# Attention's mean as a rank-one float32r product, and token numbers in buffers of their own, in a conv, attention and expert kernel

## The chip, the cores and the metric
The kernel runs on one core of a Trainium2 chip, in one launch. The metric is the device time of one execution in microseconds (us), as the median of several runs. The core's engines are TensorE (PE in the profile, with its weight loads as PEld), VectorE (DVE), ScalarE (ACT), GpSimd (POOL) and SyncE (SP, here a queue of DMAs). Each engine works through its own instructions in order, and they wait for each other by semaphores.

## What is computed
The input is x of shape (8, 56, 56, 256) in float32: 8 images of 3136 tokens with 256 channels. Cut to what matters:

```python
# layer 0: 32 paths of 1x1 conv (256 to 4), 3x3 conv (4 to 4), 1x1 conv (4 to 256), each with batch norm and relu
x = relu(sum_over_paths(conv3(conv2(conv1(x)))) + x)
# layer 1: attention with a matrix per image and head
t = x.reshape(8, 3136, 256)
n = (t - mean(t)) / sqrt(var(t) + 1e-5)           # over the 256 channels of a token
k = v = layernorm of n over each of 8 heads of 32 channels
kv = einsum('bhnd,bhne->bhde', k, v) / N
t = t + einsum('bhnd,bhde->bhne', n, kv) + n
# layer 1: mixture of 8 experts, 2 per token
n = (t - mean(t)) / sqrt(var(t) + 1e-5)
out = t + n + sum over the token's two experts of weight * (gelu(n @ w1[e] + b1[e]) @ w2[e] + b2[e])
```

The mean in the first normalisation is the one that the title speaks of: n = (t - mean) * r, so that n @ A = r * (t @ A - mean * (column sums of A)).

## The kernel before
The tokens go through in chunks: 7 chunks per image of 448 tokens each, 56 in all. A chunk is four groups of 112 tokens, which lie in 112 partitions. The work is a software pipeline over slots. Slot s holds the third conv of chunk s, the first conv of chunk s+2, the second conv of chunk s+1, the end of chunk s-1 (`end_steps`: transposes to tokens, head statistics, sums of k times v into `kvs`), the attention of chunk s-8 (`attn_steps`), the routing of tokens (`route_steps`) and some expert tiles (`moe_steps`). The instructions of PE, ACT and DVE are issued in an order written by hand: each step has a place between 0 and 1 in its slot (the table `places`, L614 on), and the steps of a slot are sorted by it. SP and POOL aren't in that list; their order follows from the program's.

In `end_steps`, `begin` stores the chunk channel-wise to DRAM (`tTs`) and `turn` stores it token-wise (`ts`). `variances` forms each token's statistics on DVE: `mu`, the sum of a token's eight head means, then `sd`, whose root POOL takes with a power (L793), or DVE by Newton steps in the last image. A slot before its attention, `fetch` brings `tT` and `X` back.

`image_steps` makes, once per image, the table `tab` that attention multiplies with: for each half f of the channels 256 columns of the image's matrix A plus the identity, with the column mean taken off, and 16 columns for the router. As A has blocks of 32x32 on its diagonal, half f has real entries in its own 128 columns; the other 128 hold only the negative column mean, which carries the token's mean.

`attend(k)` is attention for one group of 112 tokens: two matmuls into one PSUM tile (L983), then DVE scales and adds into X (L987), and ACT copies the 16 router columns to `lg` (L991):

```python
for f in range(NF):
    nc.tensor.matmul(ps, tT[:, f, k * T : (k + 1) * T], tables_of[b][:, f, :],
                     start=(f == 0), stop=(f == NF - 1))
```

The routed tokens are scattered by POOL as rows of 259 numbers (256 values, two weights, the token number) into DRAM regions by expert (L1163, `regions<-pay`). An expert tile is 256 such rows. `take_rows` loads them into a buffer `rows` of 8 (L1354, two tiles ahead), `take_weights` loads the expert's weights (L1364, one tile ahead, 4 buffers `w`), `tile_in` transposes (L1375) and names the token numbers in the rows buffer as the scatter's index, `tile_mid` and `tile_out` multiply (L1415, L1431, L1435), ACT writes `y` (L1439, 4 buffers), and `tile_add` lets POOL add the rows of y into the output at their token numbers (L1453, two scatters per tile). Only tiles that may be partial (the last 30 of 210) get an `index` tile of their own, made from the token numbers and a mask. After slot 56 there is no convolution any more; slots 57 to 64 hold attention of the last image with expert tiles, and then the remaining tiles follow.

A few names of size: T = 112, KT = 4, NF = 2, P = 128, C = 256, E = 8, CH = 448, HC = 32.

Of the kernel before, what the change touches and what calls it, by code (L numbers as in the profile page):

```python
# [8 lines left out]
F32 = mybir.dt.float32  # L9
# [16 lines left out]
def kernel(  # L26
# [30 lines left out]
    HC = 32  # L57
# [650 lines left out]
    def end_steps(s):  # L708
# [59 lines left out]
        def variances():  # L768
# [8 lines left out]
            dm = small([T, KT, NH], "hdm")  # L777
            nc.vector.tensor_reduce(mu, m, AX.X, ALU.add)
            nc.vector.scalar_tensor_tensor(
                dm, mu[:, :, None].to_broadcast([T, KT, NH]), -1.0 / NH, m,  # L780
# [63 lines left out]

    tables_of = {}

    def image_steps(b):
# [8 lines left out]
        def rows():  # L856
            v["kv"] = kvs.pop(b)

            v["rows"] = [
                one.tile([P, P], F32, tag=tag, name=f"{tag}_{b}") for tag in ("Arow", "At")  # L860
            ]
            for f in range(NF):
                nc.vector.tensor_scalar_mul(v["rows"][f], ident, ones_of(f))

        def along():
            ps = v["ps"] = ps_mm.tile([P, NF, P], F32, tag="mm", name=f"sv_{b}")
            for f in range(NF):
                nc.tensor.matmul(ps[:, f, :], ones_f, v["rows"][f], start=True, stop=True)
            v["A"] = one.tile([P, NF, P], F32, tag="A", name=f"A_{b}")

        def keys(f):
            A = v["A"][:, f, :]
            vw, vb = vw_b[:, f * P : (f + 1) * P], vb_b[:, f * P : (f + 1) * P]
            nc.vector.tensor_mul(A, v["kv"][:, f, f : f + P], vw)
            nc.vector.scalar_tensor_tensor(A, vb, ones_of(f), A, op0=ALU.mult, op1=ALU.add)
            nc.vector.tensor_scalar_mul(A, A, kw_c[:, f : f + 1])

        def values(f):  # L880
            A = v["A"][:, f, :]
            vw, vb = vw_b[:, f * P : (f + 1) * P], vb_b[:, f * P : (f + 1) * P]
            t = one.tile([P, P], F32, tag="At", name=f"At_{b}_{f}")
            nc.vector.tensor_mul(t, vw, v["ps"][:, f, :])
# [10 lines left out]
        def turn():  # L895
# [3 lines left out]
            for f in range(NF):  # L899
                nc.tensor.matmul(ps[:, f, :], mean_of, A[:, f, :], start=True, stop=True)  # L900
                nc.tensor.transpose(pt[:, f, :], A[:, f, :], ident)

        def matrix():
            A, ps = v["A"], v["cs"]
            AT = v["AT"] = one.tile([P, NF, P], F32, tag="AT", name=f"ATs_{b}")
            tab = v["tab"] = one.tile(
                [P, NF, C + 2 * E], F32, tag="tab", name=f"tab_{b}", bufs=2
            )
            nc.vector.tensor_copy(AT, v["pt"])
            for f in range(NF):  # L910
                for g in range(NF):
                    dst = tab[:, f, g * P : (g + 1) * P]
                    if f == g:
                        nc.vector.tensor_sub(dst, A[:, g, :], ps[:, g, :])
                    else:
                        nc.vector.tensor_scalar_mul(dst, ps[:, g, :], -1.0)
                nc.vector.tensor_copy(tab[:, f, C + E :], rwc[:, f, :])

# [19 lines left out]
        def centered():  # L938
            tab = v["tab"]
            for f in range(NF):  # L940
                nc.vector.tensor_sub(tab[:, f, C : C + E], v["AR"][:, f, :], v["pm"][:, :E])
            tables_of[b] = tab

# [7 lines left out]

    fetched, Xs, pays, logits = {}, {}, {}, {}

    def fetch(a):
        ts, tTs = spilled.pop(a)
        X = attn.tile([T, KT, C], F32, tag="X", name=f"X_{a}")
        tT = attn.tile([P, NF, CH], F32, tag="tT", name=f"tT_{a}")
        nc.sync.dma_start(out=tT, in_=tTs)
        nc.sync.dma_start(out=X, in_=ts)
        fetched[a] = tT  # L960
        Xs[a] = X

    def attn_steps(a):
# [15 lines left out]
        def attend(k):  # L979

            ps = ps_mm.tile([T, C + 2 * E], F32, tag="mm", name=f"at_{a}_{k}")
            for f in range(NF):
                nc.tensor.matmul(  # L983
                    ps, tT[:, f, k * T : (k + 1) * T], tables_of[b][:, f, :],
                    start=(f == 0), stop=(f == NF - 1),
                )
            nc.vector.scalar_tensor_tensor(  # L987
                X[:, k, :], ps[:, :C], rs1[:, k : k + 1], X[:, k, :],
                op0=ALU.mult, op1=ALU.add,
            )  # L990
            late.append(lambda: nc.scalar.copy(lg[:, k, :], ps[:, C:]))  # L991
            if k:
# [346 lines left out]
    def empty_rows(e):  # L1339
        pad = slots.tile([P, 2, ROW], F32, tag="rows", name=f"pad_{e}", bufs=8)  # L1340
        nc.gpsimd.memset(pad, 0.0)
# [8 lines left out]
    def take_rows(i):  # L1350
        row = entry(i, 0, E * CAPR - TR)
        z = slots.tile([P, 2, ROW], F32, tag="rows", name=f"rows_{i}", bufs=8)
        region = regions[slot_of[i][2]]
# [15 lines left out]
    def tile_in(i):  # L1369
# [12 lines left out]
        low = slot_of[i][3]  # L1382
        if low is not None:
            index = slots.tile([P, 2], I32, tag="index", name=f"index_{i}", bufs=12)
            past = slots.tile([P, 2], I32, tag="past", name=f"past_{i}", bufs=2)
# [278 lines left out]
```

## Time and profile before

| what | before |
|---|---|
| median of 3 runs | 3093.45 us (3087.57 to 3095.67) |
| the profiled execution | 3092.02 us |
| its span, first to last instruction | 3090.3 us |
| instructions | 53454 |
| mean granted TensorE clock | 0.972 |
| attention matmuls L983 | x896, 258.2 us busy |
| X update on DVE, L987 | x224, 476 ns median |
| rows loads and weight loads | x210 each, 259.0 and 513.0 KB |
| scatters of y, L1453 | x420 |

The times are of one execution. An instruction's duration in the profile is not its price on an engine that pipelines: PE's matmuls of some 400 ns overlap. What a group costs is read from the distance between starts, or from the chain of waits. A row of waits names the waiting instruction, what released it, the sum, the number of times and the longest.

### The profile page before, as it was taken

To read this page: it belongs to the slowest core of one execution; us is meant where nothing else is said; L and a number is where in the kernel's file an instruction comes from. 1 tells how busy PE (TensorE), PEld (TensorE's weight loads), DVE (VectorE), ACT (ScalarE), POOL (GpSimd) and SP (SyncE) were. 2 spreads that over 40 slices of the span, in tenths; PEclk is the share of its full clock that TensorE was granted. 3 is DMA by queue.
4 is the path that set the end of the run, shared out by engine and by line. 5 is a ranking of instruction groups with operands and counts; after the bars stand their busy time and mean duration, and the time that the engine had idled before them with its cause. 6 is when DMAs were issued, how large, how long until landed. Compare 5 with 4: busy or idle time off the path is not lost.

```text
span 3090.3 us, 53454 instructions
## 1 busy us (share of the span) xinstructions
PE 2875.4 (93%) x16677; PEld 1645.2 (53%) x16677; DVE 2124.4 (69%) x5532; ACT 1920.2 (62%) x3859; POOL 1800.1 (58%) x1333
## 2 busy tenths in 40 slices
PE   7999898888999999999999999999999997997798
PEld 3334443433455555555555555555555554776687
DVE  6877778788777777787777777787778784544000
ACT  4666566556666666667766666666666764554355
POOL 2332344445465765756766666576664556676677
PEclk8999999889999999999999999999999999998899
DMA  3534344436456777677776776767766666998897
GB/s 101 151 118 129 115 141 134 129 98 198 140 158 185 186 193 188 177 198 190 193 193 164 197 197 171 200 168 199 198 171 175 184 169 157 228 254 201 201 236 172
DMA packets 321708, 537.53 MB, mean 174 GB/s; under 512 B 40192, under 2 KB 231824, under 8 KB 321424
## 3 DMA queue, kind: packets, MB, share of 16 engines
q1 hardware_dynamic: 238464, 429.89, 45.6%
q0 software_dynamic: 82368, 103.47, 18.6%
q8 instruction: 133, 2.18, 0.3%
q14 instruction: 151, 1.24, 0.1%
q10 hardware_dynamic: 592, 0.76, 0.1%
HBM read 248.01 MB, written 192.55 MB: 143 GB/s over the span
## 4 chain that ended last, share of the span: by engine, by line
PE 72%; DVE 8%; ACT 6%; POOL 5%; DMA 5%; issue 4%; SPq 0%; ACTq 0%; POOLq 0%; DVEq 0%
PE c L660 14%; PE su L681 13%; PE ph L1415 11%; PE py L1435 9%; PE at L983 7%; PE kv L829 3%; PE c L324 3%; ACT r L665 3%; POOL hsd L793 3%; PE te L1375 3%; PE c L288 2%; DVE r L668 2%; PE py L1431 2%; DMA w<-Wd 2%; DMA out_dram<-y,rows 2%
## 5 line engine op out<-in xcount | busy, mean ns | idle before, releaser
L668 DVE SCALAR_TENSOR_TENSOR r<-c,nb,r 128x448 f32<-128x448 f32 x1792 | 1128.3, 677 | 401.2 <-ACT r L665 395.5
L665 ACT ACTIVATE r<-c,b3t 128x448 f32<-128x448 f32 x1792 | 1036.6, 634 | 342.6 <-PE c L660 338.1
L1453 POOL DMA_INDIRECT out_dram<-y,rows x360 | 567.0, 1575 | 415.6 <-ACT y L1439 262.8
L660 PE MATMUL c<-hl,W3hl 64*128 64x448 f32 x3584 | 684.9, 427 | 32.5 <-ACT r L665 18.7
L1163 POOL DMA_INDIRECT regions<-pay,rrowi x448 | 428.5, 957 | 308.9 <-PE c L660 172.8
L660 PEld LDWEIGHTS c<-hl,W3hl 64*128 64x128 f32 x3584 | 324.3, 188 | 490.6 <-issue 207.7
L681 PE MATMUL su<-r,gather 128*32 128x448 f32 x3584 | 532.2, 564 | 36.3 <-DVE r L668 32.5
L1415 PE MATMUL ph<-eT,w 128*128 128x256 f32 x1680 | 454.5, 402 | 40.2 <-DMA w<-Wd 24.0
L1439 ACT ACTIVATE y<-py,rows 128x256 f32<-128x256 f32 x420 | 196.9, 473 | 442.0 <-PE py L1435 364.9
L1435 PE MATMUL py<-w,hT 128*128 128x256 f32 x1680 | 432.8, 382 | 0.0
L1415 PEld LDWEIGHTS ph<-eT,w 128*128 128x128 f32 x1680 | 301.2, 194 | 173.0 <-issue 45.8
L793 POOL TENSOR_TENSOR hsd<-hsd,half 112x36 f32<-112x36 f32 x49 | 302.7, 6178 | 88.0 <-DVE hsd L791 84.1
L754 POOL TENSOR_TENSOR norm<-t,hmean 112x512 f32<-112x512 f32 x112 | 115.5, 1057 | 361.0 <-DVE hmean L743 220.9
L1419 ACT ACTIVATE hT<-ph,w 128x256 f32<-128x256 f32 x420 | 198.1, 476 | 187.7 <-PE ph L1415 130.9
L1435 PEld LDWEIGHTS py<-w,hT 128*128 128x128 f32 x1680 | 292.1, 192 | 29.3
L983 PE MATMUL at<-tab,tT 128*112 128x272 f32 x896 | 258.2, 411 | 7.1 <-ACT r L665 5.9
L681 PEld LDWEIGHTS su<-r,gather 128*32 128x32 f32 x3584 | 97.2, 109 | 218.7 <-issue 101.7
L1431 PE MATMUL py<-b2hl,own 128*128 128x256 f32 x420 | 182.2, 434 | 11.6 <-ACT lg L991 7.8
L983 PEld LDWEIGHTS at<-tab,tT 128*112 128x112 f32 x896 | 148.3, 179 | 81.5 <-issue 27.7
L987 DVE SCALAR_TENSOR_TENSOR X<-at,rs,X 112x256 f32<-112x256 f32 x224 | 107.0, 478 | 107.2 <-PE at L983 106.6
L1431 PEld LDWEIGHTS py<-b2hl,own 128*128 128x128 f32 x420 | 80.5, 192 | 141.8 <-issue 48.0
L324 PE MATMUL c<-R,W2t 96*32 96x448 f32 x1344 | 149.3, 546 | 0.1
(263 smaller groups left out, 3063.1 us busy)
## 6 DMA issues: line engine op xcount, KB each, us to landing
w<-Wd SPq DMA_DIRECT2D x210, 513.0 KB
rows<-regions SPq DMA_DIRECT2D x210, 259.0 KB
xi<-in_x_dram SPq DMA_DIRECT2D x56, 448.0 KB
hl<-hi SPq DMA_DIRECT2D x112, 224.0 KB
tTs<-xT SPq DMA_DIRECT2D x56, 448.0 KB
ts<-t SPq DMA_DIRECT2D x56, 448.0 KB
tT<-tTs SPq DMA_DIRECT2D x56, 448.0 KB
X<-ts SPq DMA_DIRECT2D x56, 448.0 KB
```

The costliest lines, as they stand in the source:

```text
L324: nc.tensor.matmul(ps[0][32 * g : 32 * g + 32, :CH], W2t[:, g, dy, :], R[:, g, :].rearrange("q (r w) -> q r w", w=W58)[:, dy : dy + ROWS, ...
L660: product = nc.tensor.matmul(tiles[g][:, :CH], W3hl[rows, ab, cg, :], hl[rows, ab, :], start=True, stop=True)
L665: nc.scalar.activation(r, tiles[0][:, :CH], AF.Relu, bias=b3t[:, cg, 2 * ab : 2 * ab + 1])
L668: nc.vector.scalar_tensor_tensor(r, tiles[1][:, :CH], nb3[:, cg, 2 * ab + 1 : 2 * ab + 2], r, op0=ALU.max, op1=ALU.add,)
L681: nc.tensor.matmul(ps[32 * c4 : 32 * c4 + 32, :CH], gather, unit.pop((s, 4 * u + c4)), start=(ab == 0), stop=(ab == NQ - 1),)
L793: nc.gpsimd.tensor_tensor(sd, sd, half[:T, :].rearrange("q (k h) -> q k h", k=KT), ALU.pow)
L983: nc.tensor.matmul(ps, tT[:, f, k * T : (k + 1) * T], tables_of[b][:, f, :], start=(f == 0), stop=(f == NF - 1),)
L1163: ins = nc.gpsimd.indirect_dma_start(out=regions[n], out_offset=bass.IndirectOffsetOnAxis(ap=v["row_i"][:, (m - group[0]) * KT + k, n : n ...
L1415: nc.tensor.matmul(ps, w[:, f * C + hf * P : f * C + (hf + 1) * P], eT[:, f, :], start=(f == 0), stop=(f == NF - 1),)
L1431: nc.tensor.matmul(ps, own.to_broadcast([P, P]), b2hl, start=True, stop=False)
L1435: nc.tensor.matmul(ps, hT[:, f, h * P : (h + 1) * P], w[:, (NF + f) * C : (NF + f + 1) * C], start=False, stop=(f == NF - 1),)
L1453: ins = nc.gpsimd.indirect_dma_start(out=out_rows, out_offset=at, in_=y[:, h, :], in_offset=None, compute_op=ALU.add, **partial,).ins
```

## The change
Attention's table is split. The mean's part becomes a product of its own: one float32r matmul whose stationary side holds, per token, the sum of head means as a rounded part and its remainder (`totals`, rows 0, 1, 32 and 33, all else zero), and whose moving side holds the negative column sums of A, rounded in rows 0 to 31 and the remainder in rows 32 to 63 (`less`, 272 columns with zeros under the router's). The rest of the table shrinks to 144 columns for each half: its own 128 and the router's 16. The two halves write overlapping stretches of the PSUM tile, columns 0 to 143 and 128 to 271, with the router's columns in the middle. `totals` are two buffers, zeroed once.

The rounded sums are made by DVE in `variances`, stored by SP to DRAM (`us`, 2 x 448, element by element as tokens lie across partitions), and loaded twice into `totals` by `fetch`.

In the tail, from slot 57 on, tiles that can't be partial get their token numbers copied by DVE to an `index` buffer (20 of them instead of 12), and the rows buffers go from 8 to 7.

```diff
@@ variances
             nc.vector.tensor_reduce(mu, m, AX.X, ALU.add)
+            mine = small([T, 2, KT], "hsum2")
+            nc.vector.tensor_copy(mine[:, 0, :].bitcast(F32R), mu)
+            nc.vector.tensor_tensor(
+                mine[:, 1, :].bitcast(F32R), mu, mine[:, 0, :], ALU.subtract
+            )
+            us = spill.tile([2, CH], F32, tag="us", name=f"us_{s}")
+            spilled[s] += (us,)
+            nc.sync.dma_start(out=us.rearrange("v (k q) -> q v k", q=T), in_=mine)
@@ image_steps
+    WT = P + 2 * E
+    WM = C + 2 * E
+    def router_of(tab, f):
+        return tab[:, f, P:] if f == 0 else tab[:, f, : 2 * E]
...
+            tab = v["tab"] = one.tile([P, NF, WT], F32, tag="tab", name=f"tab_{b}", bufs=2)
+            v["A"] = [tab[:, 0, :P], tab[:, 1, 2 * E :]]
...
             nc.vector.tensor_copy(AT, v["pt"])
+            less = v["less"] = one.tile([P, WM], F32R, tag="less", name=f"less_{b}", bufs=2)
             for f in range(NF):
-                for g in range(NF):
-                    dst = tab[:, f, g * P : (g + 1) * P]
-                    if f == g:
-                        nc.vector.tensor_sub(dst, A[:, g, :], ps[:, g, :])
-                    else:
-                        nc.vector.tensor_scalar_mul(dst, ps[:, g, :], -1.0)
-                nc.vector.tensor_copy(tab[:, f, C + E :], rwc[:, f, :])
+                mine = less[:, f * WT : f * WT + P]
+                nc.vector.tensor_scalar_mul(mine, ps[:, f, :], -float(HC))
+                nc.vector.scalar_tensor_tensor(
+                    mine[32:64], ps[32:64, f, :], -float(HC), mine[32:64].bitcast(F32),
+                    op0=ALU.mult, op1=ALU.subtract,
+                )
+                nc.vector.tensor_copy(router_of(tab, f)[:, E:], rwc[:, f, :])
+            nc.vector.tensor_scalar_mul(less[:, P:WT], ident[:, : 2 * E], 0.0)
@@ fetch
+    totals = [const.tile([P, CH], F32R, name=f"totals_{n}") for n in range(2)]
...
         nc.sync.dma_start(out=tT, in_=tTs)
         nc.sync.dma_start(out=X, in_=ts)
+        for n in range(2):
+            nc.sync.dma_start(
+                out=totals[a % 2][32 * n : 32 * n + 2, :].bitcast(F32), in_=us
+            )
@@ attend
-            ps = ps_mm.tile([T, C + 2 * E], F32, tag="mm", name=f"at_{a}_{k}")
+            ps = ps_mm.tile([T, 2 * WT], F32, tag="mm", name=f"at_{a}_{k}")
+            tab, less = tables_of[b]
+            nc.tensor.matmul(
+                ps[:, :WM], totals[a % 2][:, k * T : (k + 1) * T], less, start=True, stop=False
+            )
             for f in range(NF):
                 nc.tensor.matmul(
-                    ps, tT[:, f, k * T : (k + 1) * T], tables_of[b][:, f, :],
-                    start=(f == 0), stop=(f == NF - 1),
-                )
+                    ps[:, f * P : f * P + WT], tT[:, f, k * T : (k + 1) * T], tab[:, f, :],
+                    start=False, stop=(f == NF - 1),
+                )
+            mine = X[:, k, :].rearrange("q (f c) -> q f c", c=P)
             nc.vector.scalar_tensor_tensor(
-                X[:, k, :], ps[:, :C], rs1[:, k : k + 1], X[:, k, :],
-                op0=ALU.mult, op1=ALU.add,
-            )
-            late.append(lambda: nc.scalar.copy(lg[:, k, :], ps[:, C:]))
+                mine, ps.rearrange("q (f c) -> q f c", c=WT)[:, :, :P], rs1[:, k : k + 1],
+                mine, op0=ALU.mult, op1=ALU.add,
+            )
+            late.append(lambda: nc.scalar.copy(lg[:, k, :], ps[:, P:WT]))
@@ empty_rows, take_rows
-        z = slots.tile([P, 2, ROW], F32, tag="rows", name=f"rows_{i}", bufs=8)
+        z = slots.tile([P, 2, ROW], F32, tag="rows", name=f"rows_{i}", bufs=7)
@@ tile_in
         index = [z[:, h, C + 2 :].bitcast(I32) for h in range(2)]
         low = slot_of[i][3]
-        if low is not None:
-            index = slots.tile([P, 2], I32, tag="index", name=f"index_{i}", bufs=12)
+        if apart and low is None:
+            index = slots.tile([P, 2], I32, tag="index", name=f"index_{i}", bufs=20)
+            nc.vector.tensor_copy(index, z[:, :, C + 2].bitcast(I32))
+            index = [index[:, h : h + 1] for h in range(2)]
+        elif low is not None:
+            index = slots.tile([P, 2], I32, tag="index", name=f"index_{i}", bufs=20)
```

More of the change, by code (lines that the diff above doesn't have):

```diff
@@ L857, in rows @@
             v["kv"] = kvs.pop(b)
-            v["rows"] = [
-                one.tile([P, P], F32, tag=tag, name=f"{tag}_{b}") for tag in ("Arow", "At")
-            ]
+            AT = v["AT"] = one.tile([P, NF, P], F32, tag="AT", name=f"ATs_{b}")
             for f in range(NF):
-                nc.vector.tensor_scalar_mul(v["rows"][f], ident, ones_of(f))
+                nc.vector.tensor_scalar_mul(AT[:, f, :], ident, ones_of(f))
         def along():
@@ L867, in along @@
             for f in range(NF):
-                nc.tensor.matmul(ps[:, f, :], ones_f, v["rows"][f], start=True, stop=True)
-            v["A"] = one.tile([P, NF, P], F32, tag="A", name=f"A_{b}")
+                nc.tensor.matmul(ps[:, f, :], ones_f, v["AT"][:, f, :], start=True, stop=True)
+            tab = v["tab"] = one.tile([P, NF, WT], F32, tag="tab", name=f"tab_{b}", bufs=2)
+            v["A"] = [tab[:, 0, :P], tab[:, 1, 2 * E :]]
         def keys(f):
-            A = v["A"][:, f, :]
+            A = v["A"][f]
             vw, vb = vw_b[:, f * P : (f + 1) * P], vb_b[:, f * P : (f + 1) * P]
@@ L880, in values @@
         def values(f):
-            A = v["A"][:, f, :]
+            A = v["A"][f]
             vw, vb = vw_b[:, f * P : (f + 1) * P], vb_b[:, f * P : (f + 1) * P]
-            t = one.tile([P, P], F32, tag="At", name=f"At_{b}_{f}")
+            t = v["AT"][:, f, :]
             nc.vector.tensor_mul(t, vw, v["ps"][:, f, :])
@@ L899, in turn @@
             for f in range(NF):
-                nc.tensor.matmul(ps[:, f, :], mean_of, A[:, f, :], start=True, stop=True)
-                nc.tensor.transpose(pt[:, f, :], A[:, f, :], ident)
+                nc.tensor.matmul(ps[:, f, :], mean_of, A[f], start=True, stop=True)
+                nc.tensor.transpose(pt[:, f, :], A[f], ident)
         def matrix():
[L904 to L907, printed above, removed]
-            )
+            ps = v["cs"]
+            AT, tab = v["AT"], v["tab"]
             nc.vector.tensor_copy(AT, v["pt"])
+            less = v["less"] = one.tile([P, WM], F32R, tag="less", name=f"less_{b}", bufs=2)
             for f in range(NF):
-                for g in range(NF):
-                    dst = tab[:, f, g * P : (g + 1) * P]
-                    if f == g:
-                        nc.vector.tensor_sub(dst, A[:, g, :], ps[:, g, :])
-                    else:
-                        nc.vector.tensor_scalar_mul(dst, ps[:, g, :], -1.0)
-                nc.vector.tensor_copy(tab[:, f, C + E :], rwc[:, f, :])
+                mine = less[:, f * WT : f * WT + P]
[6 more added lines that the diff above has]
+            nc.vector.tensor_scalar_mul(less[:, P:WT], ident[:, : 2 * E], 0.0)
         def router():
@@ L940, in centered @@
             for f in range(NF):
-                nc.vector.tensor_sub(tab[:, f, C : C + E], v["AR"][:, f, :], v["pm"][:, :E])
-            tables_of[b] = tab
+                nc.vector.tensor_sub(
+                    router_of(tab, f)[:, :E], v["AR"][:, f, :], v["pm"][:, :E]
+                )
+            tables_of[b] = (tab, v["less"])
         return [
@@ L952 @@
     fetched, Xs, pays, logits = {}, {}, {}, {}
+    totals = [const.tile([P, CH], F32R, name=f"totals_{n}") for n in range(2)]
+    for t in totals:
+        nc.vector.tensor_scalar_mul(
+            t, ident[:, :1].to_broadcast([P, CH]), 0.0
+        )
     def fetch(a):
-        ts, tTs = spilled.pop(a)
+        ts, tTs, us = spilled.pop(a)
         X = attn.tile([T, KT, C], F32, tag="X", name=f"X_{a}")
@@ L1339, in empty_rows @@
     def empty_rows(e):
-        pad = slots.tile([P, 2, ROW], F32, tag="rows", name=f"pad_{e}", bufs=8)
+        pad = slots.tile([P, 2, ROW], F32, tag="rows", name=f"pad_{e}", bufs=7)
         nc.gpsimd.memset(pad, 0.0)
```

## The prediction
> **What bounds the kernel now.** I read the page first, then the busy time by stretch, the chain of waits in order of time, the waits of SP by stretch, and the timeline of single stalls. The first two lines below are the engines' shares and the granted clock from the page; the next are busy times by stretch (length; PE, PEld, DVE, ACT and POOL busy with their instruction counts; granted clock, DMA share, GB/s).
>
> ```profile
> PE 2875.4 (93%) x16677; PEld 1645.2 (53%) x16677; DVE 2124.4 (69%) x5532; ACT 1920.2 (62%) x3859; POOL 1800.1 (58%) x1333
> ...
> PEclk8999999889999999999999999999999999998899
> ...
> 300.00:800.00 500.00, 440.31 (x2508) 201.31 (x2508) 404.34 (x1005) 301.07 (x580) 221.50 (x154) 0.93 0.45 134
> ...
> 1500.00:2300.00 800.00, 784.39 (x4734) 434.42 (x4733) 603.94 (x1512) 539.12 (x1088) 523.85 (x361) 1.00 0.70 188
> ...
> 2870.00:2970.00 100.00, 87.31 (x415) 73.70 (x416) 2.61 (x16) 43.99 (x96) 67.28 (x48) 0.93 0.91 216
> 2640.00:2870.00 230.00, 196.15 (x1012) 167.30 (x1012) 106.38 (x486) 113.54 (x272) 162.46 (x126) 0.93 0.89 226
> 3000.00:3075.00 75.00, 75.00 (x400) 66.64 (x399) 4.79 (x29) 44.98 (x91) 58.56 (x39) 1.00 0.88 213
> ```
>
> There are four regimes. A slot is the stretch between the first L660 matmuls of two chunks. From about 829 to 2574 us (36 slots with conv, attention and expert tiles) PE has 98% and nothing else is above 76%: PE time is the time. From 304 to 829 (12 slots without tiles) PE idles 12% and loses clock. From 2640 to 2970 it idles 46.6 us of 330 at clock 0.93. From 3000 on it never idles.
>
> The chain of waits gives each group's length up to the next group's start, which is PE's real price (a matmul's own duration of some 400 ns is mostly pipeline depth):
>
> ```profile
> 2631.69 1.80 PE kv L829 x16
> 2713.59 0.92 PE at L983 x4
> 3002.03 0.12 PE py L1431
> 3004.43 1.73 PE ph L1415 x8
> ```
>
> A float32 matmul is two instructions. At 256 columns one costs 1.73/8 = 0.216 us, at 272 0.92/4 = 0.230, at 129 1.80/16 = 0.1125. The float32r matmul of 256 columns (L1431) is one instruction of 0.12.
>
> The tail's stalls start on SP's queue (waiter, what it waits for: us in all, times, longest), first for 2640 to 2840 and then from 2840 on; then POOL's scatters with start and duration:
>
> ```profile
> SPq L1354 <- DMA out_dram<-y,rows: 74.5, 19, 13.4
> ...
> SPq L1354 <- DMA out_dram<-y,rows: 88.1, 22, 10.6
> ...
> 2777.30 0.94 POOL L1163 DMA_INDIRECT regions<-pay,rrowi  x1 [0.30 <-DMA regions<-pay,rrowi]
> 2778.54 0.94 POOL L1163 DMA_INDIRECT regions<-pay,rrowi  x1 [0.30 <-issue]
> ...
> 2787.93 1.57 POOL L1453 DMA_INDIRECT out_dram<-y,rows  x1 [0.30 <-issue]
> 2789.80 1.57 POOL L1453 DMA_INDIRECT out_dram<-y,rows  x1 [0.30 <-issue]
> 2792.45 0.58 PE L1431 MATMUL py<-b2hl,own 128*128 128x256 f32 x1 [7.77 <-ACT lg L991]
> ```
>
> SP cannot load rows for tile n until the scatter of tile n-8 has landed, because that scatter reads its token numbers out of the rows buffer. The weights of a tile stand behind the rows on SP, so PE then waits for them. The last 30 tiles, which already have an index buffer of their own, run without such a wait at one tile in 4.13 us (3000.30 to 3004.43 in the chain).
>
> **The Trainium skill.** "FP8 and Floating Point Precision", TensorE Precision Notes: true FP32 takes four passes, a reduced form truncates the 4-byte value. "TensorE: Matmul & The Clock Gate", Back-to-back issue gap: N/2.4 + 2.5 ns a pass when warm. The trace agrees: two passes per instruction give 215.8, 229.2 and 110.0 ns against 216, 230 and 112.5 measured; one pass of 256 gives 109 against 120. The same page, LDWEIGHTS: columns/1.2 ns, so 93 ns for the 112 columns here, which a 122 ns matmul covers; kv's 128 weight columns under 129 moving ones show the cover. "DMA: Bandwidth & Descriptors", Specifications: below 512 B a transfer becomes a read-modify-write. The trace has 4-byte packets (19,824 on SP's queue, nearly all semaphore writes, median 9 ns) and one load of 4-byte elements (L470, 412 ns on SP), but no 4-byte data store.
>
> **The change, part by part.** The sums are made against the profiled execution, 3092.0 us with a span of 3090.3; the median of the runs is 1.4 above it.
>
> 1. PE in attend. Removed: 2 float32 matmuls of 272 columns, 0.92 us. Added: one float32r of 272, 0.12 x 272/256 = 0.128 us, and two float32 of 144, four instructions at 0.1125 x 144/129 = 0.126 (0.1225 by the skill's gap), so 0.49 to 0.50. Sum 0.62: 0.30 us less per attend, 1.2 per chunk, 67 over 56 chunks. Were float32r two passes, 0.11 more and 43 us in all; L1431 speaks against it. The extra first load of weights after a column-tiled group (0.92 becomes 1.10 at 1515.22 in the chain) is paid once before and once after.
>  By regime: 36 slots x 1.2 = 43; I take 90%, 39, since PE idles 2% there and shorter PE work opens a few waits. Slot 56: 1. The 12 early slots: 14 at most. There PE often waits for DVE's r (24.4 us, longest 5.2), behind DVE's own wait for POOL's root of hsd (58.9 us over the kernel), so I take 4. The 7 tail chunks (8 us) count in part 4.
>
> 2. The mean's road. DVE gets two 112x4 operations before that root, 0.17 + 0.03 us each by the neighbouring small rows: 0.4 us a slot, hidden behind PE with tiles, on the path in the early slots: -2 of the 12 x 0.4 = 5. SP gets the store of 896 elements of 4 bytes. It waits for DVE in `variances`; behind it on SP stand hl (which waited for DVE's hi 233.4 us anyway) and in about half the slots the next w and rows, then ph and te on PE. The L470 loads drew about 500 packets per us, so an estimate is 2 us; at 10 ns the engines give 896 x 10/16 = 0.6 us. hl follows on the same rings and has some 8 us to spare before the next slot needs it. Taken: 0; bounds 0 to a rival below. SP also gets two 1.8 KB loads per chunk into `totals`; the first attend waits for them, but they are issued a slot ahead beside tT. Their buffer is freed by attends two chunks back: 0. ACT's lg copy and DVE's X update keep size and count (the update's rows now lie 144 apart): 0, at most 224 x 0.05 = 11 on DVE, hidden except in the early slots.
>
> 3. The image steps swap 4 DVE operations of 128x128 for four others, 8 times: within 1 us, 0.
>
> 4. The tail. 51 tiles get an index copy (DVE has over half its time free there). The copy waits for rows that te needs at the same place, with attention's and the plan's DVE work behind it, which also waits for PE: 0 to -3, taken 0. Rows then go back when ACT has written y, 10 to 25 us before the scatter lands, by pairing each rows load from 2800 to 2930 with y and the scatter seven tiles earlier. So SP runs ahead, and w, the base's out store and the next X come earlier. What is late next: y has 4 buffers and also waits for the scatter (ACT 54.8 us, 13 times; the 7.77 us PE gap above is this, during eight regions scatters in a row), and POOL itself: an out scatter is 1.57 + 0.30 = 1.87 us, 3.74 a tile against PE's 4.13. With 0.30 per instruction POOL needs 162.5 + 38 = 200 of the 230 us and 67.3 + 14.4 = 82 of the 100. So at most 48 us can go, and at least the five w stalls after 2880 (1.66 + 2.46 + 1.27 + 1.47 + 1.27 = 8 us) should. I take half the ceiling, 25.
>
> 5. Rows buffers 8 to 7. The 129 tiles before the copies still free rows by the scatter. Up to slot 54 seven buffers leave 6 us or more between scatter issue and reuse, against some 3 us of landing; only around 2600 is one load held, about 12 us, 26 us ahead of its te. Bounds 0 to -8, taken -2.
>
> Sum: 39 + 1 + 4 - 2 + 25 - 2 = 65. 3092.0 - 65 = 3027; with the 1.4 to the median, 3028.
>
> **Rivals.**
> - The tail gives nothing: POOL's order of scatters, y and the last plan set it. For: POOL at 87% there, and the 7.77 us gap. Against: the SP waits of 162 us in all. Then 3093.4 - 40 = 3053.
> - PE's saving doesn't arrive: the loop PE, ACT, DVE over c and r paces a slot. For: DVE and ACT gain no time, and DVE is up to 0.88 of a slot. Against: slots at 0.2 us of PE idle. With a quarter of it and the tail, 3093.4 - 10 - 25 = 3058.
> - More than forecast: the tail reaches POOL's floor and the clock lost between 304 and 829 (39 us) partly comes back: 3093.4 - 44 - 48 - 12 = 2989.
> - Slower: the 4-byte stores. Each ring serves 56 per chunk in order, with hl behind them. Up to 8/56 = 143 ns each the slack takes it; above that every 10 ns is 0.56 us a slot, 31 us over 56 slots. At about 164 ns the 65 us are gone; at 180 ns the time is 3028 + 37 x 3.1 = 3143. For: no such store is in the trace, and the skill says it is read-modify-write. Against: 4-byte and 32-byte packets last 7 to 10 ns, 1 KB ones 46 to 58.
>
> **How the numbers follow.** Forecast 0.57, tail nothing 0.14, PE saving lost 0.12, more 0.09, slower 0.08. The forecast's own range is 3005 to 3050 (tail 5 to 45, early -8 to +12, main 32 to 43). To leave out no more than 2 in 10 the range takes in both middle rivals with their spread and the edge of the better one: 2995 to 3066. Less than 0.3% (9 us) can't be told from no change: faster 0.90, same 0.02 (where several of the gains fail together), slower 0.08.
>
> **What would show it.** Part 1: the float32r group of 224 at 0.12 to 0.13 us in the chain and at x4 at 0.50; the slots between 829 and 2574 shorter by about 1.1 us each. Part 2: SP's store of us near 0.5 us, its packets near 10 ns, hl not later. Part 4: no wait of the rows load for out_dram from the 130th tile on, PE idle from 2640 on well under 47 us, POOL over 90% there. I am wrong if the busy share of PE in the middle falls by as much as its work did, if the tail keeps its length while ACT's wait for y grows, or if 4-byte packets are over 140 ns.

## The result, and the profile after

The changed kernel takes 3074.67 us (median of 6 runs, 3071.33 to 3075.55) against 3094.56 of the kernel before on the same chip: ratio 0.9935, interval 0.9925 to 0.9945. The forecast was 65 us less, measured are 20. The profiled execution takes 3074.19 us, its span is 3072.3.

Busy time and instructions of each engine, from the page after:

```profile
PE 2842.7 (93%) x16901; PEld 1649.8 (54%) x16901; DVE 2143.1 (70%) x5705; ACT 1915.4 (62%) x3859; POOL 1798.8 (59%) x1333
```

The same view by stretch (length; PE, PEld, DVE, ACT, POOL busy with counts; clock, DMA share, GB/s):

```profile
300.00:800.00 500.00, 432.99 (x2540) 201.74 (x2536) 404.99 (x1016) 298.38 (x573) 218.32 (x152) 0.92 0.49 135
1500.00:2300.00 800.00, 780.02 (x4851) 439.38 (x4848) 614.56 (x1560) 544.85 (x1100) 526.72 (x363) 1.00 0.77 189
2640.00:2870.00 230.00, 199.18 (x1078) 173.70 (x1077) 94.80 (x476) 114.93 (x282) 166.45 (x130) 0.93 0.93 241
2870.00:2970.00 100.00, 88.75 (x430) 75.43 (x429) 11.59 (x46) 43.69 (x102) 68.55 (x46) 0.93 0.93 213
```

In the middle PE is busy 97.5% where it was 98%. Its work per slot fell by 2.5%, but its busy share hides most of what happened: the starts below show groups that take longer with little idle time in the record. In the tail PE idles 42 us of 330, where it idled 46.5, and the DMA share rose from 0.89 and 0.91 to 0.93. The mean granted clock is 0.968, where it was 0.972: the stretches below full clock, each counted by the share of speed that it lacks, cost 98.5 us in all, where they cost 87.5.

Where the time went is told by starts. The table is worked out from the first L660 matmul of slots 8, 20 and 55 in each trace (us):

| trace | up to slot 8 | slots 8 to 19 | slots 20 to 54 | from 55 to the end |
|---|---|---|---|---|
| before | 304.2 | 525.0 | 1697.3 | 563.8 |
| after | 307.0 | 529.2 | 1681.0 | 555.2 |
| difference | +2.8 | +4.2 | -16.3 | -8.6 |

The 35 slots of the middle were to bring 1.2 us each, 42. The distance from each matmul's start to the next one's, summed by group over these slots, shows what came of it: attend 134.5 to 104.6 us; the expert tiles' groups (te, ph, py, and pyb, which is py at L1431 before and L1463 after) 573.4 to 561.5, some 8 of these 12 in the distance to an attend that follows them. So the 42 us are there. The third convolution (c, L660) grew from 405.5 to 426.5 and su (L681, which sums its paths) from 272.6 to 277.6: 26 us came back.

Slot by slot the picture is steadier than these sums. In 32 of the 35 slots both traces have the full clock; there the change brings 0.47 us a slot on average, 15.2 in all, of the 1.2 that attend gives.

How the rest comes back is seen in the chain of waits, here in one slot, the same in both kernels. Before:

```profile
1548.85 0.92 PE tx L277 x8
1549.77 0.78 PE c L660 x4
1550.55 1.07 PE su L681 x8
1551.62 0.61 PE c L660 x4
1552.22 1.10 PE at L983 x4
1553.33 1.52 PE c L288 x4
...
1554.86 0.69 DVE r L668
...
1555.59 0.46 PE c L660
```

And after:

```profile
1519.68 0.12 PE at L1006
1519.81 0.49 PE at L1010 x4
...
1546.81 0.92 PE tx L277 x8
1547.72 0.80 PE c L660 x3
1548.52 0.67 ACT r L665
1549.25 0.57 issue
1549.82 0.68 DVE r L668
...
1551.15 0.60 DVE xT L687
...
1552.82 0.69 DVE r L668
1553.55 0.46 PE c L660
```

The price of attend is as forecast (0.12 for the float32r instruction and 0.49 for the four float32 ones). But from tx to the last c it is 6.74 us in both kernels: the chain now leaves PE for ScalarE's and VectorE's r, and what PE saves at the attend in between it waits longer for the last r. That r stands behind VectorE's own queue. These are the two r operations around it on VectorE (start, duration), before and then after:

```profile
1551.26 1.28 DVE L668 SCALAR_TENSOR_TENSOR r<-c,nb,r 128x448 f32<-128x448 f32 x2 [0.64 <-ACT r L665]
...
1554.86 1.27 DVE L668 SCALAR_TENSOR_TENSOR r<-c,nb,r 128x448 f32<-128x448 f32 x2
```

```profile
1549.22 1.28 DVE L668 SCALAR_TENSOR_TENSOR r<-c,nb,r 128x448 f32<-128x448 f32 x2 [0.64 <-ACT r L665]
...
1552.82 1.27 DVE L668 SCALAR_TENSOR_TENSOR r<-c,nb,r 128x448 f32<-128x448 f32 x2
```

In both kernels 3.60 us lie between them, and VectorE works without a gap there (nine router operations of 112x32, 112x64 and 112x8 and an xT of 128x448). PE's last c waits for that r in both, 0.16 us before and 0.46 after. So at this place VectorE's order of work sets the length, before the change too.

The wait that part 4 wanted gone is gone. SP's queue, first 2640 to 2840, then from 2840 on (waiter, cause: us, times, longest):

```profile
SPq L1382 <- DMA out_dram<-y,rows: 6.8, 2, 4.9
...
SPq L1382 <- ACT y L1471: 9.9, 6, 2.9
```

The wait of the rows load for scatters was 162.6 us before (from 2640 on) and is 6.8 now. Of ACT's waits from 2640 on, the one for y's buffers, before and then after:

```profile
ACT y L1439 <- DMA out_dram<-y,rows: 54.8, 13, 12.2
```

```profile
ACT y L1471 <- DMA out_dram<-y,index: 100.1, 25, 11.2
```

It has nearly doubled: rows run ahead, and y stands in their place. Both sizes belong to this trace: in e5 and e6 below, the same two kernels on another chip, the rows' wait is 57.5 and then 5.7 us, and y's 14.5 and then 32.7.

### The profile page after: what moved, and what is told of

Its sections match the earlier page's. It is cut to its first block, busy times and chain, and to the rows that moved or that the text cites. A ratio compares the mean times of both kernels' runs of the same rounds, so it can differ in the third digit from the quotient of the medians.

```text
span 3072.3 us, 54367 instructions
## 1 busy us (share of the span) xinstructions
PE 2842.7 (93%) x16901; PEld 1649.8 (54%) x16901; DVE 2143.1 (70%) x5705; ACT 1915.4 (62%) x3859; POOL 1798.8 (59%) x1333
## 4 chain that ended last, share of the span: by engine, by line
PE 39%; DVE 4%; DMA 3%; ACT 3%; POOL 3%; issue 3%; POOLq 0%; ACTq 0%; DVEq 0%; SPq 0%
PE ph L1447 8%; PE py L1467 7%; PE c L660 6%; PE su L681 6%; DMA out_dram<-y,index 3%; PE te L1403 2%; PE py L1463 2%; PE at L1010 2%; PE c L324 2%; PE kv L837 1%; POOL regions L1191 1%; DVE r L668 1%; ACT r L665 1%; POOL out_dram L1485 1%; ACT y L1471 1%
## 5 line engine op out<-in xcount | busy, mean ns | idle before, releaser
L660 PE MATMUL c<-hl,W3hl 64*128 64x448 f32 x3584 | 700.7, 430 | 36.4 <-ACT r L665 19.8
L1485 POOL DMA_INDIRECT out_dram<-y,rows x258 | 408.0, 1582 | 318.4 <-ACT y L1471 243.1
L660 PEld LDWEIGHTS c<-hl,W3hl 64*128 64x128 f32 x3584 | 331.2, 188 | 488.9 <-issue 215.5
L681 PE MATMUL su<-r,gather 128*32 128x448 f32 x3584 | 540.5, 566 | 43.4 <-DVE r L668 33.6
L1485 POOL DMA_INDIRECT out_dram<-y,index x162 | 251.0, 1549 | 94.1 <-issue 26.5
L681 PEld LDWEIGHTS su<-r,gather 128*32 128x32 f32 x3584 | 99.4, 109 | 231.2 <-DVE r L668 106.1
L1463 PE MATMUL py<-b2hl,own 128*128 128x256 f32 x420 | 175.1, 417 | 16.7 <-ACT y L1471 7.7
L1463 PEld LDWEIGHTS py<-b2hl,own 128*128 128x128 f32 x420 | 80.0, 190 | 145.4 <-issue 48.9
L1403 PE MATMUL te<-ident,rows 128*128 128x128 f32 x840 | 135.2, 284 | 19.4 <-ACT y L1471 18.4
```

The source lines that it names most:

```text
L660: product = nc.tensor.matmul(tiles[g][:, :CH], W3hl[rows, ab, cg, :], hl[rows, ab, :], start=True, stop=True)
L681: nc.tensor.matmul(ps[32 * c4 : 32 * c4 + 32, :CH], gather, unit.pop((s, 4 * u + c4)), start=(ab == 0), stop=(ab == NQ - 1),)
L1463: nc.tensor.matmul(ps, own.to_broadcast([P, P]), b2hl, start=True, stop=False)
L1485: ins = nc.gpsimd.indirect_dma_start(out=out_rows, out_offset=at, in_=y[:, h, :], in_offset=None, compute_op=ALU.add, **partial,).ins
```

## The experiments

The runs came in five groups, each on one chip with the kernel before beside it. Its median was 3103.9 us for e1 to e4, 3109.1 for e5 to e8, 3094.4 for e9 to e12, 3104.1 for e13 to e16 and 3109.5 for e17 and e18. Ratios are against these; stretches are compared within a group where that is possible. The second and the fourth group ran on the same chip. Where slots of the middle are compared one by one, only those count in which both traces have the full clock.

**Half of the change at a time.** e1 takes the index copies back, e2 everything but them and the 7 rows buffers.

```diff
-        if apart and low is None:
-            index = slots.tile([P, 2], I32, tag="index", name=f"index_{i}", bufs=20)
-            nc.vector.tensor_copy(index, z[:, :, C + 2].bitcast(I32))
```

> The mean product with its road, rows buffers 7, without the index copies of the tail. Theory (DVE paces the middle: of the 43 us that PE saves between 829 and 2574 us, 17 arrive; early slots lose 4; the tail part is worth 8): 8 us above the changed kernel, so about 3083, ratio 0.996 to before. Rival (the tail's copies gave nothing and the 8 us in the tail are the 7 chunks' shorter matmuls): 3075, as the changed kernel.

> Before with only the index copies and rows buffers 7. Theory: the middle as before, the tail's wait moves from the rows load to y's four buffers; 5 to 10 us off, 3084 to 3089. Rival (the copies are what gave the whole 20 us, the mean product nothing): 3075.

Measured: e1 3103.05 us, 1.0002 (0.9992 to 1.0011); e2 3104.74, 1.0004 (0.9995 to 1.0013). The middle is 1687.5 in e1 and 1699.3 in e2, so the mean's product does bring 12 us there; the time from slot 55 on is 573.3 and 577.0, where the first pair of traces had 563.8 and 555.2. Neither half alone moved the time of the whole. Neither the kernel before nor the whole change was traced on this chip, so these tails have no reference of their own. In e2 the rows' wait for scatters from 2640 on is down to 2.2 us, and the whole is no faster: the wait that part 4 wanted gone can go without any gain.

**The mean's road.** e3 leaves out the store and the loads of the mean's sums; e4 has the two DVE operations and the store in `inverse`, after the root.

```diff
@@ e3
-            nc.sync.dma_start(out=us.rearrange("v (k q) -> q v k", q=T), in_=mine)
...
-        for n in range(2):
-            nc.sync.dma_start(
-                out=totals[a % 2][32 * n : 32 * n + 2, :].bitcast(F32), in_=us
-            )
@@ e4, in inverse
+            nc.vector.tensor_copy(mine[:, 0, :].bitcast(F32R), total)
+            nc.vector.tensor_tensor(
+                mine[:, 1, :].bitcast(F32R), total, mine[:, 0, :], ALU.subtract
+            )
+            nc.sync.dma_start(out=v["us"].rearrange("v (k q) -> q v k", q=T), in_=mine)
```

> The changed kernel without the store of us and the two loads of totals (totals stay zero, so the token's mean is left out); DVE's two operations stay. Theory (DVE): within 3 us of the changed kernel, 3072 to 3078, though the DMA share of the middle falls back from 0.77 to about 0.70 and the mean of a 4104-byte packet from 239 to about 210 ns. Rival (the 4-byte stores slow the loads and so the slots): 10 us or more faster than the changed kernel, 3065 or less.

> The changed kernel with DVE's two operations and the store of us moved from before POOL's root to behind it, where DVE waits for POOL anyway. Theory (the two operations delay r by 0.36 us a slot and start the root later): 0.2 to 0.3 us in each of 36 slots and 0.3 in the 12 early ones, 9 to 14 us faster than the changed kernel, 3061 to 3066; the sixth su group and the c group before the second half of conv2 return to their lengths of before. Rival (DMA contention, or PE itself): no change, 3072 to 3078.

Measured: e3 3092.4, 0.9971 (0.9958 to 0.9983); e4 3113.91, 1.0043 (1.0027 to 1.0059). Without the road the middle stays at 1689.0 against e1's 1687.5, so the store costs nothing there. From slot 55 on e3 takes 565.0 against 573.3, but it has the index copies that e1 lacks, so that difference isn't the road's alone. In e4 the middle is 1705.7, 18 us longer than in e1. Nearly all of that is clock: the stretches below full clock cost 22.2 us there, and 5.1 in e1; what lowered the clock isn't shown. In the 23 slots with full clock in both, the typical (median) slot is 0.27 us shorter than in e1, as the theory said (0.2 to 0.3), although single slots are up to 2.6 longer and the mean is only 0.10. So the two operations do cost something in front of the root, and the store pays for their new place: it stands on SP until the root is done, with hl and xi behind it, and PE waits 11.8 us for hl, all of it ahead of slot 20.

**The two kernels again, the operations left out, and VectorE relieved.** e5 is the kernel before, e6 the changed one. e7 stores a constant in place of the two DVE operations' result; e8 halves two reductions.

```diff
@@ e7
-            nc.vector.tensor_copy(mine[:, 0, :].bitcast(F32R), mu)
-            nc.vector.tensor_tensor(
-                mine[:, 1, :].bitcast(F32R), mu, mine[:, 0, :], ALU.subtract
-            )
+            mine = nothing
@@ e8, also for the means
-                ss, v["sq"].rearrange("q k (h c) -> q (k h) c", c=HC), AX.X, ALU.add
+                ss, v["sq"].rearrange("q k (h c) -> q (k h) c", c=HC)[:, :, : HC // 2],
+                AX.X, ALU.add
```

> The kernel before, unchanged, as a traced reference on the same chip as the next three. Ratio 1.000. Every theory: middle (slots 20 to 54) 1697 us, early slots 525; only the tail may differ from the first trace, by some 10 us, if chips differ in how fast scatters and loads land.

> The changed kernel, unchanged, as a traced reference. If the two parts add, and the mean product alone and the tail's copies alone each gave nothing on that chip, the ratio is 1.000 there; if they need each other (the copies only help once PE is ahead of POOL), 0.994 as at first. Middle 1681, early 529.

> The changed kernel without DVE's two operations in variances; the store of us sends a tile of zeros instead (the token's mean is left out), so SP no longer waits there for DVE. Theory (DVE is the second bound and the two operations are its overflow): 0.36 us in most middle slots, so the middle 1668 to 1672 instead of 1681 and the c group before conv2's second half shorter; early 525; 10 to 15 us faster than the changed kernel. Rival (the give-back has nothing to do with these two): within 3 us of the changed kernel.

> The changed kernel with DVE's two long reductions per chunk (head sums and squares, 1.21 us each) over half of each head's channels, so the statistics are not the reference's; 1.2 us of DVE time per slot less, nothing else. Theory (DVE is what takes back PE's saving in the middle): c and su groups shrink by most of the 26 us they gained, middle about 1660, 20 us or more faster than the changed kernel. Rival (ACT's half of the loop, or DMA): middle unchanged within 4 us.

Measured: e5 1.0006 (0.9993 to 1.0018); e6 3100.98, 0.9974 (0.9962 to 0.9985), so on this chip the change is worth 8 us; e7 3221.7, 1.0373 (1.0347 to 1.0398); e8 3064.11, 0.9864 (0.9848 to 0.9879). The middle: 1702.5, 1691.2, 1681.7, 1670.0.

e7's stores have nothing to wait for, so SP ran them ahead, and this priced them by themselves. SP's queue (start, duration), then what PE waited for up to slot 8, then the DMA's packets while these stores ran:

```profile
69.26 49.77 SPq L784 DMA_DIRECT2D us<-nothing  x15
```

```profile
PE c L660 <- DMA hl<-h: 115.3, 4, 40.4
```

```profile
DMA packets 14545, 0.09 MB, mean 2 GB/s; under 512 B 14542, under 2 KB 14542, under 8 KB 14542
```

15 stores of 896 elements in 49.77 us are 3.3 us a store, or 59 ns an element on each of 16 rings, and PE waited 115.3 us for hl behind such stores; e7 reaches slot 8 134 us later than e6. e7's middle is 9.5 us under e6's, and the typical slot 0.26 us shorter, as in e4. This fits a price of the two operations (0.33 us of VectorE), but e7 also took SP's wait away.

**One chip for the operations and y's buffers.** e9 is the changed kernel; e10 is the kernel before with e8's relief; e11 has y in 5 buffers and rows in 6; e12 has the two operations on GpSimd.

```diff
@@ e11
-            hidden[i].append(work.tile([P, 2, C], F32, tag="y", name=f"y_{i}", bufs=4))
+            hidden[i].append(work.tile([P, 2, C], F32, tag="y", name=f"y_{i}", bufs=5))
@@ e12
-            nc.vector.tensor_copy(mine[:, 0, :].bitcast(F32R), mu)
-            nc.vector.tensor_tensor(
+            nc.gpsimd.tensor_copy(mine[:, 0, :].bitcast(F32R), mu)
+            nc.gpsimd.tensor_tensor(
```

> The changed kernel, unaltered, as the reference of this group: its ratio to the kernel before was 0.9935 in the first comparison and 0.9974 on another chip. Here 0.993 to 0.998. In the middle (the 35 slots 20 to 54, between first matmuls of the first convolution) 1681 to 1692 us.

> The kernel before, with the two DVE reductions over 1024 elements of a chunk (sums and sums of squares per head) reduced to half their elements, as in e8 on the changed kernel; the output differs. DVE work falls by 2 x 0.53 us a slot. With it the four cases with and without the change, and with and without the relief of DVE, are complete. Theory (DVE is a second bound in the middle, and takes what PE gives): in the kernel before, PE is the later one, so the relief brings little there: middle 0 to 10 us shorter than the kernel before's 1697 to 1703, so that between this kernel and e8 (1670) lie 25 to 35 us, most of the 42 that the price of attend promises; whole kernel 0.995 to 1.000. Rival (the relief shortens a chain in either kernel alike, and the lost saving is lost to something else, as slower transfers): middle 21 us shorter here too, ratio 0.989 to 0.992.

> The changed kernel with y in 5 buffers instead of 4, rows in 6 instead of 7 (for room), and the index copies for all tiles (by GpSimd ahead of the tail, by VectorE in it). Theory (in the tail the wait for rows was replaced by ACT's wait for a free y, 100 us in 25 waits from 2640 on): that wait falls to under half, PE's waits for te and py fall, and the stretch from slot 55 to the end becomes 5 to 15 us shorter than in e9. Rival (GpSimd's scatters pace the tail, whatever buffers there are): the wait moves to another place and the stretch stays within 3 us.

> The changed kernel with the two added operations of 112x4 in variances on GpSimd instead of VectorE, ahead of GpSimd's root of hsd, for which it waits about 2.8 us there. The store waits for GpSimd then. Theory (DVE's two operations cost some 9.5 us in the middle and 4 early, since DVE is the second bound): if GpSimd does both in under 2.8 us, the middle is 7 to 11 us shorter than e9 and the early slots 2 to 4. If GpSimd takes longer than it has, the root of hsd is later by the excess, the early slots lose 12 times the excess, and the middle gains less. Rival (the cost was the store's, not the operations'): no shorter than e9 anywhere.

Measured: e9 3074.49, 0.9934 (0.9921 to 0.9946), with the stretches of the first trace within 1 us; e10 3076.14, 0.9941 (0.9929 to 0.9953), between the ranges of theory and rival, middle 1696.4 in an execution that is the slowest of its six (3085.76); e11 3122.25, 1.0087 (1.0073 to 1.0102); e12 3075.56, 0.9944 (0.9927 to 0.9961), middle 1680.0 against e9's 1681.0.

GpSimd did both operations of e12 in the gap ahead of its root (start, duration, operation):

```profile
1770.13 0.21 POOL L780 CAST hsum<-hmu 112x4 fp32r<-112x4 f32 x1 [1.34 <-DVE hmu L778]
1770.42 0.20 POOL L781 TENSOR_TENSOR hsum<-hmu,hsum 112x4 fp32r<-112x4 f32 x1
1771.33 6.14 POOL L802 TENSOR_TENSOR hsd<-hsd,half 112x36 f32<-112x36 f32 x1 [0.71 <-DVE hsd L800]
```

So VectorE was rid of 0.33 us a slot, and the middle gained 1 us (0.02 in the typical slot): the theory's 7 to 11 failed here, and the two operations' price in the middle lies between 1 us (e12) and 9.5 (e7). Why GpSimd doing them gives back what e4 and e7 gained isn't shown. Slots 8 to 19 lost 3.0, with 8.5 us more lost to the clock, and the stretch ahead of them gained 2.8.

In e11 the copies for all tiles, which GpSimd makes in the slots, held up other work there: the middle is 1709.3, and PE waits 14.3 us in it for GpSimd's norm. The tail can still be looked at. ACT's wait for y from 2640 on, e9 and then e11:

```profile
ACT y L1471 <- DMA out_dram<-y,index: 124.6, 31, 11.1
```

```profile
ACT y L1471 <- DMA out_dram<-y,index: 104.7, 25, 9.7
```

A fifth buffer takes 20 us off the wait, and the stretch from slot 55 on is not shorter (562.2 against 555.6). As rows have one buffer less at the same time, this says only that the trade brought nothing, not that y's buffers are no limit.

**ScalarE's share, and the DMA engines in the tail.** e13 is the changed kernel, e14 is e8 again, e15 halves ScalarE's squares as well, e16 has every second tail tile use its neighbour's weights.

```diff
@@ e15
-                    sq[:, :, f * P : (f + 1) * P], norm[:, :, f * (P + 1) : f * (P + 1) + P],
+                    sq[:, :, f * P : (f + 1) * P].rearrange("q k (h c) -> q k h c", c=HC)[
+                        :, :, :, : HC // 2
+                    ],
+                    heads(norm)[f][:, :, :, : HC // 2],
@@ e16
+        if apart and i % 2 and i - 1 in weights_of:
+            weights_of[i] = weights_of[i - 1]
+            return
         e = entry(i, 1, E - 1)
```

> The changed kernel, unaltered, as the reference on this chip: middle (slots 20 to 54) 1681 to 1692 us, from slot 55 to the end 555 to 573.

> The changed kernel with VectorE's two reductions over 1024 elements halved, as in e8; the output differs. Theory (VectorE is the second bound in the middle once attend is shorter): middle 15 to 21 us shorter than e13, where the kernel before lost only 1 us by the same relief (e10). Rival (e8's gain was the chip's): middle within 4 us of e13.

> As e14, and ScalarE's squares over the halves that are used only (two operations a slot, 0.63 us each, to about 0.4); the output differs. Theory A (what e14 leaves of the lost saving is ScalarE's, which reads c before VectorE does): the third convolution shortens by 5 us or more against e14, toward the kernel before's 405 us. Theory B (the rest is the length of the loop PE, ScalarE, VectorE, PE itself, which shorter work in between no longer covers, however much time these engines have): within 3 us of e14 in the middle.

> The changed kernel, but in the tail every second tile takes its neighbour's weights in place of loading its own 513 KB; the output differs. GpSimd's, ScalarE's and PE's instructions stay. Theory (the DMA engines are what holds the tail now: share 0.93 from 2640 to 2870): the stretch from slot 55 to the end 15 us shorter or more, y's buffers come free sooner since the scatters land sooner, ACT's wait for y at under 70 us (from 100 to 125), and the middle unchanged. Rival (order and number of GpSimd's scatters): that stretch within 5 us, ACT's wait for y as it was, DMA share down to 0.75 to 0.8.

Measured: e13 3095.94, 0.9977 (0.9969 to 0.9985); e14 3060.88, 0.9864 (0.9837 to 0.9890); e15 3071.57, 0.9889 (0.9868 to 0.9911); e16 3086.13, 0.9941 (0.9925 to 0.9956). The middle: 1689.4, 1668.9, 1669.4, 1689.4. ScalarE's squares are worth nothing there, though the relief is small: ScalarE is busy 32.6 us a slot in e14 and 32.3 in e15. In e16 the stretch from slot 55 on is 7.3 us shorter (566.2 to 558.9), between the two theories. One stretch of the tail, e13 and then e16:

```profile
2840.00:2940.00 100.00, 82.10 (x406) 69.51 (x405) 28.38 (x130) 42.69 (x97) 71.94 (x56) 0.88 0.87 216
```

```profile
2840.00:2940.00 100.00, 86.76 (x429) 73.88 (x428) 29.44 (x132) 46.80 (x102) 71.77 (x55) 0.90 0.76 169
```

The DMA share falls by 0.11, PE does 6% more in the same time, and GpSimd is as busy as before. ACT's wait for y from 2640 on is 41.9 us in e13 and 20.8 in e16. The clock is a rival in this pair of traces: from slot 55 on 49.2 us are lost to it in e13 and 40.5 in e16, more than the 7.3. Over all runs it is not: e16 is 10 us faster by the medians, and the mean clocks, 0.9648 and 0.9654, are worth some 2 us. So the transfers hold a part of the tail, not all.

**The relief with and without the change on one chip.** e17 is e10's kernel, e18 is e8's.

> As e10: the kernel before with VectorE's two reductions halved; the output differs. Theory (VectorE became late through the change): less gain than e18 over e13 in the middle, 0 to 5 us below the kernel before's 1697 (on a chip with 3094 us for the kernel before) or 1702 (3104 to 3109). Rival: 15 us or more below.

> As e14: the changed kernel with the same relief; the output differs. Theory: middle 25 to 35 us shorter than e17, in place of the 12 to 16 that the change brings there without the relief, and the whole 15 us or more below e17. Rival: 12 to 16 us in the middle, as without the relief.

Measured: e17 3097.07, 0.9960 (0.9947 to 0.9973); e18 3078.28, 0.9896 (0.9869 to 0.9922). The middle is 1696.2 and 1675.7. With VectorE relieved the change brings 20.5 us there, and 19 in the whole (the medians' difference). Without the relief it brought 16.3 in the first pair and 11.3 between e5 and e6. By slots with full clock it is 0.63 us a slot with the relief, and 0.47 and 0.44 without it. The theory's 25 to 35 was too much, the rival's 12 to 16 too little. The third convolution takes 406.3 us in e17 and 422.9 in e18: most of what it gives back, it gives back with VectorE relieved too.

## Why the forecast's sign was right and its size wrong

**Part 1, the price: right.** "Sum 0.62" an attend; the chain shows 0.12 and 0.49, and the groups' starts show the 42 us over 35 slots. The Trainium skill gives true FP32 four passes and says of a reduced form only that it truncates ("FP8 and Floating Point Precision", TensorE Precision Notes); that float32r needs no more than one here is the trace's word, 0.12 us for 272 columns. One slip of the working changes nothing: its three figures for two passes take the gap of 2.5 ns once an instruction, not once a pass as it says; the other way each is 2.5 ns longer.

**Part 1, what arrives: the step that failed.** "36 slots x 1.2 = 43; I take 90%, 39, since PE idles 2% there." 16.3 us arrived, 11.3 on another chip: 27 to 39% of 42 in place of 90. The chips hardly differ in this: by slots with full clock it is 0.47 us a slot in the first pair and 0.44 between e5 and e6, and the rest is clock and a few slots. PE's busy share is no measure of what a shorter group brings: the groups around it took longer while PE stayed busy in the record, and the sign that was named for this, a falling busy share, showed 0.5 points only. 26 us came back at the third convolution and su.

VectorE holds a part: its relief is worth 1 to 6 us in the middle before the change (e10 against the first trace, e17 against e5, across groups) and 14 to 21 after it (e8 and e14; e18 across groups). By slots with full clock that is 0.14 to 0.18 us before and 0.43 to 0.48 after. The rest, about 16 us at the convolution, stands with VectorE's two reductions relieved, and with a little of ScalarE's squares too. VectorE isn't acquitted of it: the relief left the rest of its work as it was, and in the slot shown above it is the router's operations that stand ahead of the r PE waits for. Sorted by what the traces name as the releaser, 8 of the 21 us that the convolution gained end with VectorE's r, 7 of them after 2 us or more of VectorE work without a gap, and some 6.5 with ScalarE's r. That the trip PE, ScalarE, VectorE, PE, with VectorE's other work inside it, is what attend used to cover is argued from this and not shown: no run shortened that trip or moved the router's operations. It is the rival "PE's saving doesn't arrive", which had 0.12.

**Part 1, early slots: wrong.** Forecast were 4 us of gain there less 2 for part 2. Measured are 4.2 us of loss, and 2.8 up to slot 8. Attend is 13.8 us shorter there, and the second and third convolutions and su are 17.5 longer; 5 us are granted clock (39.3 us lost before, 44.4 after), a term that the forecast put at nothing. Over the whole execution it is 11 us, 4 of them from slot 55 on; as PE also waits in these stretches, what they cost in time can be less.

**Part 2, the road.** "Hidden behind PE" doesn't hold for the two operations in e4 and e7, where the typical slot is 0.27 and 0.26 us shorter without them ahead of the root. It would hold in e12, where VectorE is rid of them and the typical slot gains 0.02. They cost between 1 and 9.5 us of the middle, which the runs don't settle. They stand, as forecast, ahead of the root (start, duration, operation in the trace after):

```profile
1766.47 0.18 DVE L778 TENSOR_REDUCE hmu<-hmean 112x4 f32<-112x32 f32 x1
1766.68 0.17 DVE L780 CAST hsum<-hmu 112x4 fp32r<-112x4 f32 x1
1766.88 0.16 DVE L781 TENSOR_TENSOR hsum<-hmu,hsum 112x4 fp32r<-112x4 f32 x1
1766.96 0.18 DVE L787 SCALAR_TENSOR_TENSOR hdm<-hmu,hmean 112x32 f32<-112x32 f32 x1
```

Back to back in e7 a store takes 3.3 us of the rings, above the estimate of 2 and far above 0.6, and at 59 ns an element well under the 143 that the slack takes. In the changed kernel itself its 4-byte packets are short (9 ns); what rises is the time of all packets, by 3.0 us a slot on each ring in the middle, 2.3 of it in other transfers' packets of 1024 and 4104 bytes. So the store's 0 was right for the middle (e3), and the rival of a slower kernel fell. e4 shows that the slack ahead of hl is not large: with the store held until after the root, PE waits for hl.

**Part 4, the tail: wrong in size.** "I take half the ceiling, 25." The rows' wait went as forecast, from 162.6 to 6.8 us for scatters, and 8.6 us were gained, within the bounds of 8 and 48; between e5 and e6 it is 3.2. These needn't be the index copies': attend's own saving in the 7 tail chunks was priced at 8, and e2, which has the copies alone, is no faster. What was named as late next, y's 4 buffers, did become late (54.8 to 100.1 us), and a fifth buffer at the rows' cost brought nothing (e11). What part 4 didn't count are the DMA engines: their share was 0.89 and 0.91 before, so by this measure about 10% was left, and is 0.93 after. Taking transfers away brought some 7 us (e16). The 42 us that PE still idles between 2640 and 2970 aren't explained by any one run.

**Part 5** wasn't tried by itself. **Chance:** the time fell in the gap between the two middle rivals and no change, 9 us above the range. The range joined each rival to the other part's full gain; both parts falling short together was given too little.

No run here beats the changed kernel with the whole computation in it; the relieved ones leave part of it out.

## What to carry to other kernels

A PE that is busy 98% of a stretch can still be waiting: before forecasting what a shorter group brings, add up starts to starts by group and see whether the neighbours' groups are at their own price or above it. Shorter filler work between two halves of a dependent loop can give back what it saves, so ask what that round trip takes, and what other work each engine does inside it. Compare slot by slot, and leave out the slots with a lowered clock: the same slots agreed on two chips where the sums didn't. When a wait on a buffer goes, look at the share of the DMA engines in that stretch before looking for the next buffer.

## What the runs showed of the hardware

- Back to back (e7), a store of 4-byte elements to DRAM costs 59 ns an element and ring (3.3 us for 896 on 16 rings); in the skill's terms it is a transfer below 512 B ("DMA: Bandwidth & Descriptors", Specifications), and this is its price here. It shows in the DMA share from 829 to 2526 us: 0.69 before, 0.76 after, and 0.69 without the road (e3), at 185 to 187 GB/s.
- In e12 the root of 112x36 takes GpSimd 6.14 us, a copy of 112x4 only 0.21.
- The change is worth 0.9935 and 0.9934 (first pair, e9) where the kernel before takes 3094 us, and 0.9974 and 0.9977 (e6, e13) on another chip, where it takes 3104 to 3109. The intervals don't overlap: a ratio from one chip is that chip's. In the time of either kernel the granted clock is a large part of the difference: from slot 55 on 32.9 and 37.0 us are lost to it in the first pair, and 45.0 and 50.8 in e5 and e6, where that stretch is 12 and 17 us longer.
